# A two-dimensional DFT in array quadrants, and the engines' order from the scheduler's other machine model

## The chip, the cores and the metric

The kernel runs on one core of one Trainium2 chip. The metric is the device time of one execution in microseconds (us), smaller is better. A core has five engines that run side by side, each with its own instruction queue: TensorE (PE in the profile: matrix multiplications, whose weight loads are listed as PEld), VectorE (DVE), ScalarE (ACT), GpSimd (POOL), and SyncE (SP), which here only issues DMA transfers. An engine executes its queue in order. When its next instruction needs something that is not there yet, it waits, and everything behind that instruction waits with it.

## The reference, cut to what matters

The input is 32 images of 96 channels, 56 x 56 pixels, float32. Two layers follow one another.

```python
# layer 0
h = silu(bn(conv1x1(x, w1)))                 # 96 -> 576 channels
h = silu(bn(depthwise3x3(h, w2)))
s = sigmoid(w_b @ silu(w_a @ mean(h)))       # squeeze and excitation
x = x + bn(conv1x1(h * s, w3))               # 576 -> 96
# layer 1
mag = abs(rfft2(x))                          # first DFT
ca  = channel_attention(mag)                 # 96 numbers for an image
s   = stack(mean_c(x), l2_c(x), resize(mean_c(mag)))
s   = conv_1x15(conv_15x1(s))                # each of the 3 planes by itself
sa  = sigmoid(mix(relu(conv3x3(s))))         # one 56 x 56 map for an image
y   = x * ca * sa
freq_e = resize(mean_c(abs(rfft2(y))))       # second DFT
aux = concat(y, coord, freq_e)
offset, gate, base = conv3x3(aux), gate_net(aux), conv3x3(y)
z   = (1 - gate) * base + gate * deformable_conv3x3(y, offset)
out = relu(batchnorm_over_all_images(z) + x)
```

What the change touches is `abs(rfft2(.))`, computed twice for each image, 64 times in all, and the order in which the instructions of the whole kernel stand on four of the five engines.

## The kernel before

**Stages.** `body` (line 1332) calls `layers`, which computes everything up to z for all images, and then `normalise`, which reads z and x back, applies the batch normalisation and writes the output. A third function, `gather_block`, serves offsets too large for the fast path; with these inputs it is not executed.

**Three streams in `layers`.** The main loop goes over 224 bands (7 bands of 8 rows for each of 32 images), and over two halves of a band. A half loads its interpolation weights (`weights_load`, to `wc` and `wr`) and multiplies them (`weights`, VectorE, L685). `block_channels` copies 8 x 8 pixel blocks (GpSimd, L696), transposes them (TensorE, L700) and copies the result out (ScalarE, L702). `sample_tiles` interpolates the samples by matrix multiplication (TensorE, L714, ScalarE copies in L718), `pack` moves part of the samples to the spare partitions with three ScalarE copies (L725), and `deform` multiplies by the deformable kernel (TensorE, L733). The joint 3x3 convolution (L598), the base convolution (L626) and `combine` (VectorE, L772 to L775) complete the band. Between these pieces the loop steps two Python generators: `hidden`, which is layer 0 of the image two ahead (TensorE L166, ScalarE L170 and L219, VectorE L259), and `attend` for the image one ahead. So each image period holds work of three images.

**`attend` of an image.** It first projects (L321, after loads of the hidden rows `hq`). Then `dft_mag` takes the first DFT, `resized_spectrum` (L420 to L423) averages it over channels, L490 to L512 compute the channel attention, and L514 to L549 the spatial attention. The spatial part is a chain of small steps: L524, L526 and L527 on TensorE, L528 on ScalarE, three L533 with L534 on ScalarE, nine L540 with L542 on ScalarE, L544 and L546 on VectorE, L549 on TensorE, and the sigmoid (L273 on ScalarE, L274 on VectorE). Its result `sa` is sent to DRAM by a DMA of GpSimd's queue (L554), and is multiplied into the loaded pixels by GpSimd (L363, in `weigh`) for the second DFT. The row of frequency energy that follows goes to DRAM from L565 over L567 and L570 (`fqd`), and is loaded into the padded image by L589, a transfer of SyncE's queue, which the joint convolution L598 needs.

**`dft_mag`.** The 96 channels are taken as two halves of 48 that lie on the partitions side by side (2 x 56 = 112 rows of pixels). In six groups of eight channels a tile `x2` (112 x 8 x 56) is loaded. Four matmuls (L383) use two channels of `x2` as weights (112 columns) and a constant block matrix `FU` of 116 columns as the moving data: this is the DFT along one image axis. ScalarE copies the result to `s1` (L390). The transform along the other axis (L404) runs over `s1` in three steps. Each step has two parts (real and imaginary) of two matmuls that accumulate, with a 112 x 112 block-diagonal constant `GV` as weights and 464 moving columns. So in each of these matmuls half of the weights are zeros. ScalarE squares each part out of its accumulation bank (L406), and VectorE adds the two squares (L407). The square root (L410) ends the DFT. The tile `sq` of the squares and the tile `s1` have one buffer each, `x2` has three.

**What sets the order.** SyncE's queue is written out by hand: within `layers` the engine is under a manual schedule, so its transfers stand as the program emits them. The order on TensorE, VectorE, ScalarE and GpSimd is decided when the program is built. A list scheduler plays the emitted program on a model of the machine and writes, for each engine, the order in which instructions became ready; an earlier emission has the higher priority. The scheduler has two machine models with different costs, and before the change the default one is in use:

```python
    with tile.TileContext(nc) as tc:
```

Accumulation memory is shared among the streams: six banks for general use (`bank`, named `mm` in the profile), one (`acc`) for the small steps of the attention, one (`pd`) for `deform`.

Of the kernel before, what the change touches and what calls it, by code (L numbers as in the profile page):

```python
# [7 lines left out]
FP = mybir.dt.float32  # L8
I32 = mybir.dt.int32
AF = mybir.ActivationFunctionType  # L10
ALU = mybir.AluOpType
# [13 lines left out]
V = W // 2 + 1  # L25
# [35 lines left out]
NG = C // 2 // CG  # L61
KG = 3
# [52 lines left out]
def bank(p):  # L115
    return p["mm"].tile([128, 512], FP, name="mm")
# [219 lines left out]
def dft_mag(nc, p, src, gate=None):  # L336

    w = p["w"]
    hwc = src.rearrange("c (h w) -> h c w", h=H)
    s1 = p["s1p"].tile([2 * W, NP, 2 * V], FP, name="s1")
    if gate is None:
        parts = p["sq"].tile([2 * W, 2, NPB * V], FP, name="sq")[:, :, : NG * W].rearrange("p k (g w) -> p k g w", g=NG)  # L350
    x2s = []

    def load(g):
        if g < NG:
            x2 = p["x2"].tile([2 * H, CG, W], FP, name="x2")
            for half in range(2):
                c0 = half * C // 2 + g * CG
                nc.sync.dma_start(x2[half * H : (half + 1) * H], hwc[:, c0 : c0 + CG])
            x2s.append(x2)

    def weigh(g):
        if gate is not None and g < NG:
            nc.gpsimd.tensor_tensor(x2s[g], x2s[g], gate.unsqueeze(1).to_broadcast([2 * H, CG, W]), ALU.mult)  # L363

    def sums(g):
        sq = bank(p)[: 2 * H, : CG * W].rearrange("h (c w) -> h c w", c=CG)
        nc.scalar.activation(sq, x2s[g], AF.Square)
        for k, t in enumerate((x2s[g], sq)):
            nc.vector.tensor_reduce(parts[:, k, g], t.rearrange("h c w -> h w c"), AX.X, ALU.add)

    for g in range(3):
        load(g)
    for _ in range(2):
        yield
    weigh(0)
    weigh(1)
    yield
    if gate is not None:
        yield
    for g in range(NG):  # L380
        pt = bank(p)
        for i in range(CG // 2):
            nc.tensor.matmul(pt[: 2 * W, i * 4 * V : (i + 1) * 4 * V],  # L383
                             x2s[g][:, 2 * i : 2 * i + 2, :].rearrange("h c w -> h (c w)"), w["FU"],
                             start=True, stop=True)
        if gate is None:
            sums(g)
        weigh(g + 2)
        load(g + 3)
        nc.scalar.copy(s1.rearrange("p (h q) u -> p h q u", h=2)[:, :, g * CG // 2 : (g + 1) * CG // 2],  # L390
                       pt[: 2 * W, : 2 * CG * V].rearrange("p (q h u) -> p h q u", h=2, u=2 * V))
        yield
    if gate is None:
        p["sums"] = p["sp"].tile([2 * H, 2, W], FP, name="sums")
        nc.vector.tensor_reduce(p["sums"], parts.rearrange("p k g w -> p k w g"), AX.X, ALU.add)
    mag = s1[:, :, :V]
    for j in range(0, NP, NPB):
        n = NPB * V
        sq = p["sq"].tile([2 * W, 2, n], FP, name="sq")
        cos, sin = s1[:, j : j + NPB, :V], s1[:, j : j + NPB, V:]  # L400
        for part, first, second in ((0, (0, cos), (1, sin)), (1, (0, sin), (2, cos))):
            pt = bank(p)
            for k, (g, m) in enumerate((first, second)):
                nc.tensor.matmul(pt[: 2 * W, :n].rearrange("p (q u) -> p q u", q=NPB), w["GV"][:, g], m,  # L404
                                 start=(k == 0), stop=(k == 1))
            nc.scalar.activation(sq[:, part], pt[: 2 * W, :n], AF.Square)  # L406
        nc.vector.tensor_tensor(mag[:, j : j + NPB], sq[:, 0].rearrange("p (q u) -> p q u", q=NPB),  # L407
                                sq[:, 1].rearrange("p (q u) -> p q u", q=NPB), ALU.add)
        yield
    nc.scalar.activation(mag, mag, AF.Sqrt)  # L410
    p["magnitude"] = mag


def resized_spectrum(nc, p, mag, name, scale=None):


    m2 = p["sp"].tile([2 * W, V], FP, name=f"m_{name}")
    if scale is not None:
        nc.vector.tensor_tensor(mag, mag, scale.unsqueeze(2).to_broadcast([2 * W, NP, V]), ALU.mult)
    nc.vector.tensor_reduce(m2, mag.rearrange("p q u -> p u q"), AX.X, ALU.add)  # L420
    yield
    pf = p["acc"].tile([128, 512], FP, name="acc")
    nc.tensor.matmul(pf[:V, : 2 * W], m2, p["w"]["RT2"], start=True, stop=True)  # L423
    rs = p["sp"].tile([V, 2, W], FP, name=name)
    nc.scalar.copy(rs.rearrange("p m w -> p (m w)"), pf[:V, : 2 * W])
    p["resized"] = rs
    yield


def attend(tc, p, b, x, h2d, pooled, x1, given=False):  # L430
# [45 lines left out]
    mas = p["sp"].tile([2 * W, 2, NP], FP, name="mas")  # L476
    edge = p["sp"].tile([2 * W, NP, NE], FP, name="edge")
# [3 lines left out]
    for m in range(2):  # L481
        we = p["sp"].tile([2 * W, NP, NE], FP, name="we")
        nc.vector.tensor_tensor(we, edge, w["wa"][:, m], ALU.mult)
        nc.vector.tensor_reduce(mas[:, m], we, AX.X, ALU.add)


    qs = p["sp"].tile([2 * W, 2, 3, NP], FP, name="qs")
    for m in range(2):
        nc.vector.tensor_tensor(qs[:, m], mas[:, m].unsqueeze(1).to_broadcast([2 * W, 3, NP]), w["wb"][:, m], ALU.mult)
# [16 lines left out]
    c2 = p["sp"].tile([2 * MID, 2 * W], FP, name="c2")  # L506
# [5 lines left out]
    nc.tensor.matmul(pc[: 2 * W, 64 : 64 + NP], c2, w["cp2X"], start=True, stop=True)  # L512
    cx = p["sp"].tile([2 * W, NP], FP, name="cx")
    nc.vector.tensor_tensor(cx, pc[: 2 * W, 64 : 64 + NP], w["cp2bX"], ALU.add)  # L514
# [264 lines left out]
def constants(tc, ctx, a, p, gather=False):  # L779
# [63 lines left out]
    wa = cp.tile([2 * W, 2, NP, NE], FP, name="wa")  # L843
    wb = cp.tile([2 * W, 2, 3, NP], FP, name="wb")
    gb = cp.tile([C, 3], FP, name="gbias")
    with tc.tile_pool(name="l1w", bufs=1) as wp:
# [7 lines left out]
        ap, bp, fdh, fdw = temp("apad", 2 * W), temp("bpad"), temp("fdhX"), temp("fdwX")  # L854
        ta = wp.tile([2 * W, NP, NE], FP, name="ta")
        tb = wp.tile([2 * W, 3, NP], FP, name="tb")
        for m in range(2):
            for d in range(7):
                first = d == 0
                oa, ob = (wa[:, m], wb[:, m]) if first else (ta, tb)  # L860
                nc.vector.tensor_tensor(oa, ap[:, m, d].unsqueeze(1).to_broadcast([2 * W, NP, NE]),
                                        fdh[:, :, d : d + 1].to_broadcast([2 * W, NP, NE]), ALU.mult)
                nc.vector.tensor_tensor(ob, bp[:, m, :, d : d + 1].to_broadcast([2 * W, 3, NP]),
                                        fdw[:, :, d].unsqueeze(1).to_broadcast([2 * W, 3, NP]), ALU.mult)
                if not first:
                    nc.vector.tensor_tensor(wa[:, m], wa[:, m], ta, ALU.add)
                    nc.vector.tensor_tensor(wb[:, m], wb[:, m], tb, ALU.add)
# [41 lines left out]
def padded(nc, p, a, images):  # L909
# [3 lines left out]
    for t in yps:  # L913
        nc.gpsimd.memset(t, 0.0)
        nc.sync.dma_start(t[C : C + 4, PD : PD + H, PD : PD + W], a["coord"])
        nc.sync.dma_start(t[CA:, PD : PD + H, PD : PD + W], a["place"])
    p["s4"] = [cp.tile([H, 3, WP], FP, name=f"s4_{i}") for i in range(2)]
# [11 lines left out]
def layers(tc, a, dp, x1d, zd, stats, far):  # L929
# [8 lines left out]
    with ExitStack() as ctx:  # L938
# [7 lines left out]
        pools(tc, ctx, p, None, (("xt", 2), ("acch", 2), ("pl", 2), ("w3s", 1), ("hq", 1), ("o", 2), ("x2", 3),  # L946
# [290 lines left out]
def gather_block(tc, a, dp, x1d, zd, stats):  # L1237
# [4 lines left out]
    with ExitStack() as ctx:  # L1242
# [11 lines left out]
        pools(tc, ctx, p, None, (("x2", 3), ("ca", 1), ("s1p", 1), ("xc", 2), ("sp", 1), ("sq", 2), ("q1", 2), ("q2", 2),  # L1254
# [95 lines left out]
def _arrays(inp):  # L1350
# [39 lines left out]
    A["cp1"] = np.ascontiguousarray(cp1.reshape(2 * MID, 3, NP, 2).transpose(2, 1, 3, 0))  # L1390
    cp2 = l1["cp2_w"].reshape(NP, 2, MID)
    A["cp2X"] = np.ascontiguousarray(cp2.transpose(1, 2, 0).reshape(2 * MID, NP))
    A["cp2bX"] = np.ascontiguousarray(np.repeat(l1["cp2_b"].reshape(NP, 2).T, W, 0))
    A["twoT"] = np.kron(np.eye(2), np.ones((MID, W))).astype(f)
# [8 lines left out]
    for k in range(1, KA):  # L1403
# [13 lines left out]
    A["GV"] = np.ascontiguousarray(np.stack(  # L1417
        [np.kron(two, np.cos(t)), np.kron(two, np.sin(t)), np.kron(two, -np.sin(t))], 1).astype(f))
    A["two"] = np.kron(two, np.ones((W, 1))).astype(f)
# [8 lines left out]
    apad, bpad = np.zeros((1, 2, 7, V), f), np.zeros((2, W, 2, 3, 7), f)  # L1428
    for d in range(7):
# [3 lines left out]
        bpad[:, -np.arange(V), 1, :, d] = bp[:, 6 - d : 6 - d + V].T[:, None]  # L1433
# [4 lines left out]
    A["apad"], A["bpad"] = ends, bpad.reshape(2 * W, 2, 3, 7)  # L1438
    A["bsum"] = np.stack([bp[:, 6 - d : 6 - d + V].sum(1) for d in range(7)], -1).astype(f)[None]
    pairs = lambda v: np.repeat(v.reshape(NP, 2, 7).transpose(1, 0, 2), W, 0)  # L1440
# [7 lines left out]
    RT2 = np.zeros((2, W, 2, W), f)  # L1448
    RT2[:, np.arange(V), 0] = RT / C
    RT2[:, -np.arange(V), 1] = RT / C  # L1450
    A["RT2"] = RT2.reshape(2 * W, 2 * W)
# [37 lines left out]
```

## Time and profile before

| quantity | value |
|---|---|
| time, median of 3 runs | 9672.42 us (9670.12 to 9673.45) |
| the profiled execution's own time | 9701.68 us |
| its span | 9699.9 us |
| TensorE busy | 8626.3 us, 89% of the span |
| VectorE busy | 7237.3 us, 75% |
| ScalarE busy | 5341.9 us, 55% |
| GpSimd busy | 2531.2 us, 26% |
| granted TensorE clock, mean | 0.932 of full speed |
| column transform, L404 | 662.9 us busy, 1536 records |
| row transform, L383 | 418.1 us busy, 3072 records |

How to read it: the profile is of one execution, and its span is the sum that all its rows belong to; it lies 29 us above the median of the runs that were timed without a profile. [...] A row of a group of instructions reads: line, engine, operation, tile written and tiles read, shapes, number of records, then the busy time in us, the mean of one in ns, and the idle time of the engine just ahead of these instructions with what ended most of it. Records of matmuls overlap, so that a mean is longer than the pace at which they follow one another. A row of a timeline reads: start in us, duration in us, engine and operation with the number of records, and in brackets the idle time before it and what ended it. A row of the table by stretches gives, for each engine, busy us and the number of records, and at its end the granted clock, the share of the DMA engines' time that is busy, and GB/s. A row of the waits gives the us in all, how often, and the longest.

### The profile page before, as it was taken

Reading aid. Unit: us, or ns where it says so; the run is one execution under the profiler, and the core shown is the slowest. Engines: PE = TensorE matmul, PEld = TensorE weight load, DVE = VectorE, ACT = ScalarE, POOL = GpSimd, SP = SyncE. Lnnn points to the kernel's source line nnn. Section 1 sums busy time; section 2 is a strip of 40 time slices with the busy share of each in tenths; the row PEclk is TensorE's granted clock in tenths of the full one; section 3 lists DMA queues with packets and bytes.
Section 4 is the critical chain, followed back from the end, with each engine's and each line's share of the span. In section 5 each row is a group of like instructions: output and inputs, shape, how many; then the busy total and the mean of one; then the engine's idle time right before and its main releaser. Section 6 shows DMA issues by size and latency. Waiting matters only on the chain. (4 is left out here: it accounts for less than half of the span.)

```text
span 9699.9 us, 120622 instructions
## 1 busy us (share of the span) xinstructions
PE 8626.3 (89%) x43766; PEld 5004.7 (52%) x43766; DVE 7237.3 (75%) x6948; ACT 5341.9 (55%) x10262; POOL 2531.2 (26%) x2639
## 2 busy tenths in 40 slices
PE   6889999999999999999999999999999999999970
PEld 3455555555555555555555555555555555555540
DVE  7688777777877777787777787777778777777323
ACT  2355555555555556555555555555555555555453
POOL 0133222222222232222222222233222223322210
PEclk9899999999999999999999999999999999999985
DMA  2345555554555555555555555555545555554449
GB/s 94 107 136 143 160 153 157 157 153 138 140 158 152 157 149 148 140 144 150 153 158 154 139 139 155 153 157 155 152 138 143 151 157 157 153 146 135 128 152 417
DMA packets 1069310, 1485.39 MB, mean 153 GB/s; under 512 B 590406, under 2 KB 839958, under 8 KB 1056422
## 3 DMA queue, kind: packets, MB, share of 16 engines
q1 hardware_dynamic: 858747, 985.20, 37.3%
q10 hardware_dynamic: 153675, 329.79, 9.1%
q0 software_dynamic: 56288, 162.60, 6.8%
q8 instruction: 352, 5.77, 0.3%
q14 instruction: 248, 2.03, 0.1%
HBM read 1064.28 MB, written 412.65 MB: 152 GB/s over the span
## 5 line engine op out<-in xcount | busy, mean ns | idle before, releaser
L259 DVE SCALAR_TENSOR_TENSOR acch<-hp,w,acch 128x1512 f32<-128x1512 f32 (+1 forms) x2250 | 4314.4, 1918 | 32.8
L598 PE MATMUL mm<-yp,c_jointW 104*128 104x448 f32 x4032 | 1648.5, 561 | 6.2 <-DMA yp<-fqd 3.4
L733 PE MATMUL pd<-v,c_def 128*96 128x224 f32 (+1 forms) x6272 | 1435.2, 380 | 174.5 <-ACT v L725 147.9
L696 POOL COPY ybl<-yp 96x448 f32<-96x448 f32 x896 | 1016.6, 1161 | 2002.3 <-PE mm L700 1996.8
L733 PEld LDWEIGHTS pd<-v,c_def 128*96 128x96 f32 (+1 forms) x6272 | 1065.3, 175 | 487.7 <-ACT v L725 186.7
L166 PE MATMUL mm<-xt,w 96*128 96x392 f32 (+3 forms) x2688 | 1117.2, 553 | 132.6 <-ACT yt L702 95.9
L714 PE MATMUL mm<-wc,yt 64*96 64x144 f32 x12544 | 1113.9, 301 | 119.1 <-ACT v L718 59.3
L598 PEld LDWEIGHTS mm<-yp,c_jointW 104*128 104x128 f32 x4032 | 785.1, 196 | 802.7 <-issue 760.1
L685 DVE TENSOR_TENSOR wc<-wc,wr 128x1008 f32<-128x1008 f32 x448 | 559.3, 1248 | 776.4 <-DMA wr<-hd 767.9
L219 ACT ACTIVATE acch<-acch,sh,inv 128x1568 f32<-128x1568 f32 x288 | 487.4, 1692 | 1159.2 <-DVE acch L259 1141.5
L714 PEld LDWEIGHTS mm<-wc,yt 64*96 64x96 f32 x12544 | 847.7, 162 | 442.9 <-issue 197.7
L718 ACT COPY v<-mm 96x288 f32<-96x288 f32 (+1 forms) x2688 | 1003.1, 441 | 127.9 <-PE mm L714 85.6
L170 ACT ACTIVATE hp<-mm,sh,inv 128x392 f32<-128x392 f32 (+2 forms) x1216 | 811.6, 672 | 329.4 <-PE mm L166 280.8
L626 PE MATMUL mm<-yp,c_base0W 96*64 96x448 f32 x4032 | 914.6, 551 | 0.0
L321 PE MATMUL mm<-hq,w3s 128*96 128x392 f32 x2048 | 789.9, 532 | 126.5 <-DMA hq<-h2d 124.2
L648 POOL DMA_DIRECT2D od<-at x224 | 185.9, 830 | 2257.6 <-DVE at L644 1483.9
L725 ACT COPY v<-v 32x448 f32<-32x448 f32 x1344 | 755.1, 562 | 29.7
L404 PE MATMUL mm<-s,c_GV 112*112 112x464 f32 x1536 | 662.9, 573 | 0.0
L166 PEld LDWEIGHTS mm<-xt,w 96*128 96x128 f32 (+1 forms) x2688 | 390.5, 187 | 513.8 <-issue 289.8
L702 ACT COPY yt<-mm 128x384 f32<-128x384 f32 (+1 forms) x896 | 351.1, 441 | 463.9 <-PE mm L700 462.0
L321 PEld LDWEIGHTS mm<-hq,w3s 128*96 128x96 f32 x2048 | 336.9, 173 | 478.6 <-issue 374.4
L626 PEld LDWEIGHTS mm<-yp,c_base0W 96*64 96x64 f32 x4032 | 295.3, 135 | 527.8 <-issue 487.9
(193 smaller groups left out, 8959.1 us busy)
## 6 DMA issues: line engine op xcount, KB each, us to landing
h2d<-acch ACTq DMA_DIRECT2D x288, 784.0 KB
wc<-hd SPq DMA_DIRECT2D x896, 252.0 KB
wr<-hd SPq DMA_DIRECT2D x896, 252.0 KB
hq<-h2d SPq DMA_DIRECT2D x128, 980.0 KB
hq<-h2d SPq DMA_DIRECT2D x128, 784.0 KB
x<-x1d SPq DMA_DIRECT2D x768, 98.0 KB
ht<-od SPq DMA_DIRECT2D x224, 252.0 KB
hd<-ht ACTq DMA_DIRECT2D x224, 252.0 KB
```

The costliest lines, as they stand in the source:

```text
L166: nc.tensor.matmul(pt[p0 : p0 + w1.shape[1], : rows * W], w1, xts[hf][:, r0 * W : (r0 + rows) * W], start=True, stop=True)
L170: nc.scalar.activation(h1[lo:hi, row0 : row0 + rows, 1 : 1 + W], pt[lo:hi, : rows * W].rearrange("p (h w) -> p h w", h=rows), AF.Silu, bia ...
L259: nc.vector.scalar_tensor_tensor(acc[:, lo:hi], win, wk, acc[:, lo:hi], ALU.mult, ALU.add)
L321: nc.tensor.matmul(pts[half][:C, :EW], w3s[:, ch], hq, start=(i == 0), stop=False)
L404: nc.tensor.matmul(pt[: 2 * W, :n].rearrange("p (q u) -> p q u", q=NPB), w["GV"][:, g], m, start=(k == 0), stop=(k == 1))
L598: nc.tensor.matmul(view, weights[:, k], yp[:channels, r0 : r0 + RB, dx + PD - 1 : dx + PD - 1 + W], start=(k == 0), stop=(k == NTAP - 1))
L626: nc.tensor.matmul(pb[k % 2 * BC : (k % 2 + 1) * BC, :BW].rearrange("p (h w) -> p h w", h=RB), w["base"][:, k], yp[:C, r0 : r0 + RB, dx + ...
L696: nc.gpsimd.tensor_copy(yb[:, :, s], blocks)
L714: nc.tensor.matmul(pt[k][:C, (t - lo) * KP : (t - lo + 1) * KP], yt[ps, t], s[ps, t * KP : (t + 1) * KP], start=True, stop=True)
L718: nc.scalar.copy(v[:C, :, lo:hi, k].rearrange("c k t p -> c t k p"), pt[k][:C, : (hi - lo) * KP].rearrange("c (t k p) -> c t k p", t=hi - ...
L725: nc.scalar.copy(v[C:, 1 + 2 * i : 3 + 2 * i], v[i * QC : (i + 1) * QC, KA:])
L733: nc.tensor.matmul(out.rearrange("c q (t x) -> c t q x", x=TS), p["w"]["def"][ks, k], v[ks, k].rearrange("c t s (r x) -> c t (s r) x", r=T ...
```

## The change

It has two parts. The first is one argument in `kernel`: the list scheduler plays the program on its other machine model, so that the order on TensorE, VectorE, ScalarE and GpSimd is another one. SyncE's hand-written order stays.

The second is in `dft_mag`, with the constants that it needs. Each half of the channels now lies on 64 partitions instead of 56 (`WX`), of which the last eight are padding. The three `x2` tiles are no longer taken from a pool: they are three fixed tiles, zeroed once at the start by GpSimd and used in turn. The row transform's weights are 128 columns wide instead of 112. The column transform is divided into the four quadrants of the TensorE array: a matmul has 56 rows of one row half (`r`), writes 64 columns of one column half (`k`) and has 232 moving columns, so there are 48 of them for a DFT where there were 12, and no zero block. A step fills two banks, one for each row half, and one bank holds both parts. A square now covers one bank (464 columns, both parts), so there are still six squares and three additions for a DFT. The order of the channels changes with it, and the constants follow by `order`. The small tiles of the attention become 128 partitions high instead of 112.

```diff
+WX = 64
+NQB = 8
...
-    s1 = p["s1p"].tile([2 * W, NP, 2 * V], FP, name="s1")
+    s1 = p["s1p"].tile([2 * WX, NP, 2 * V], FP, name="s1")
...
-            x2 = p["x2"].tile([2 * H, CG, W], FP, name="x2")
+            x2 = p["x2"][p["n_x2"] % len(p["x2"])]
+            p["n_x2"] += 1
             for half in range(2):
                 c0 = half * C // 2 + g * CG
-                nc.sync.dma_start(x2[half * H : (half + 1) * H], hwc[:, c0 : c0 + CG])
+                nc.sync.dma_start(x2[half * H : (half + 1) * H, :, :W], hwc[:, c0 : c0 + CG])
             x2s.append(x2)
...
-            nc.tensor.matmul(pt[: 2 * W, i * 4 * V : (i + 1) * 4 * V],
+            nc.tensor.matmul(pt[:, i * 4 * V : (i + 1) * 4 * V],
...
     mag = s1[:, :, :V]
-    for j in range(0, NP, NPB):
-        n = NPB * V
-        sq = p["sq"].tile([2 * W, 2, n], FP, name="sq")
-        cos, sin = s1[:, j : j + NPB, :V], s1[:, j : j + NPB, V:]
-        for part, first, second in ((0, (0, cos), (1, sin)), (1, (0, sin), (2, cos))):
-            pt = bank(p)
-            for k, (g, m) in enumerate((first, second)):
-                nc.tensor.matmul(pt[: 2 * W, :n].rearrange("p (q u) -> p q u", q=NPB), w["GV"][:, g], m,
-                                 start=(k == 0), stop=(k == 1))
-            nc.scalar.activation(sq[:, part], pt[: 2 * W, :n], AF.Square)
-        nc.vector.tensor_tensor(mag[:, j : j + NPB], sq[:, 0].rearrange("p (q u) -> p q u", q=NPB),
-                                sq[:, 1].rearrange("p (q u) -> p q u", q=NPB), ALU.add)
+    n = NQB * V
+    pairs = mag.rearrange("p (r q) u -> p r q u", r=2)
+    for q0 in range(0, NP // 2, NQB):
+        sq = p["sq"].tile([2 * WX, 2, 2, n], FP, name="sq")
+        pts = bank(p), bank(p)
+        for part, first, second in ((0, (0, 0), (1, V)), (1, (0, V), (2, 0))):
+            for t, (g, u0) in enumerate((first, second)):
+                for r, k in ((0, 0), (1, 1), (0, 1), (1, 0)):
+                    rows = slice(r * WX, r * WX + W)
+                    q1 = k * NP // 2 + q0
+                    nc.tensor.matmul(pts[r][k * WX : (k + 1) * WX, part * n : (part + 1) * n].rearrange("p (q u) -> p q u", q=NQB),
+                                     w["GV"][rows, g], s1[rows, q1 : q1 + NQB, u0 : u0 + V], start=(t == 0), stop=(t == 1))
+        for r, pt in enumerate(pts):
+            nc.scalar.activation(sq[:, r].rearrange("p k n -> p (k n)"), pt[:, : 2 * n], AF.Square)
+        nc.vector.tensor_tensor(pairs[:, :, q0 : q0 + NQB], sq[:, :, 0].rearrange("p r (q u) -> p r q u", q=NQB),
+                                sq[:, :, 1].rearrange("p r (q u) -> p r q u", q=NQB), ALU.add)
         yield
     nc.scalar.activation(mag, mag, AF.Sqrt)
...
+    p["x2"], p["n_x2"] = [cp.tile([2 * H, CG, WX], FP, name=f"x2_{i}") for i in range(3)], 0
+    for t in p["x2"]:
+        nc.gpsimd.memset(t, 0.0)
     p["s4"] = [cp.tile([H, 3, WP], FP, name=f"s4_{i}") for i in range(2)]
     for t in p["s4"]:
         nc.gpsimd.memset(t, 0.0)
...
+    order = np.arange(C).reshape(2, NP // 2, 2).transpose(0, 2, 1).reshape(2, NP)
+    A["cp1"] = np.ascontiguousarray(cp1.reshape(2 * MID, 3, C)[:, :, order].transpose(3, 1, 2, 0))
...
-    A["GV"] = np.ascontiguousarray(np.stack(
-        [np.kron(two, np.cos(t)), np.kron(two, np.sin(t)), np.kron(two, -np.sin(t))], 1).astype(f))
-    A["two"] = np.kron(two, np.ones((W, 1))).astype(f)
+    gv = np.zeros((2, WX, 3, WX), f)
+    gv[:, :W, :, :W] = np.stack([np.cos(t), np.sin(t), -np.sin(t)], 1)
+    A["GV"] = gv.reshape(2 * WX, 3, WX)
...
-    with tile.TileContext(nc) as tc:
+    with tile.TileContext(nc, schedule_with_timeline_sim=True) as tc:
```

## The prediction

> **What bounds the kernel now.** I read the page first (busy totals, costly groups), then TensorE's waits, then its timeline round the two places that the change touches.
>
> ```profile
> PE 8626.3 (89%) x43766; PEld 5004.7 (52%) x43766; DVE 7237.3 (75%) x6948; ACT 5341.9 (55%) x10262; POOL 2531.2 (26%) x2639
> ...
> L733 PE MATMUL pd<-v,c_def 128*96 128x224 f32 (+1 forms) x6272 | 1435.2, 380 | 174.5 <-ACT v L725 147.9
> ...
> L404 PE MATMUL mm<-s,c_GV 112*112 112x464 f32 x1536 | 662.9, 573 | 0.0
> ```
>
> TensorE (PE) is busy 89% of the span. In the band loop, 600 to 9240 us, it is busy 8015.7 of 8640 us by the windows, so 624 us are idle, some 20 us in each image period of 285 us. VectorE is at 75% and the others are lower. The end, 9400 to 9700 us, is bound by DMA (417 GB/s in the last slice) and is untouched. So a microsecond off TensorE's work, or off its waits, in the loop is a microsecond off the time, as long as nothing new is waited for. The answers by line show what is waited for, and two rows that the change will meet:
>
> ```profile
> PE mm L321 <- DMA hq<-h2d: 124.2, 30, 7.9
> PE mm L166 <- ACT yt L702: 95.9, 40, 5.4
> ...
> PE mm L383 <- POOL x L363: 37.9, 35, 3.5
> ```
>
> ```profile
> L363 POOL TENSOR_TENSOR x<-x,sa 112x448 f32<-112x448 f32 x192 | 381.3, 2006 | 10.7 <-DMA x<-x1d 9.8
> ...
> L406 ACT ACTIVATE sq<-mm 112x464 f32<-112x464 f32 x384 | 202.3, 552 | 323.0 <-DVE s L407 235.9 <-PE mm L404 69.0 <-DVE sums L395 10.7
> ```
>
> **Part 1, the column transform in quadrants.** A float32 matmul leaves two records, and a burst of 16 records of L404 takes 6.59 us in the timeline: 0.412 us each. There are 64 DFTs (two for each of 32 images) x 24 records = 1536; 1536 x 0.412 = 633 us, all on TensorE's path. After: 64 x 48 instructions x 2 records = 6144 records of 232 columns instead of 464, so 0.206 us each. Four quadrants at once would make it 6144 / 4 x 0.206 = 316 us. One after another it would be 1266 us, two at a time 633. No quadrant pair stands in this trace; the nearest rows are two-way: L626 (two column halves) starts pairs some 7 ns apart every 381 ns, L714 (two row halves) pairs 6 ns apart every 122 ns, each the time of one. So halves do run together, in both directions. [...] By rows: a set of 16 new matmuls takes 16 x 2 / 4 x 0.206 = 1.65 us, and its evacuation two L406 squares (2 x 0.552) and one L407 addition (0.640), with hops some 2 us, through one single buffer. [...] Squares, additions and copies keep their number and size (112 to 128 partitions only), so they cost nothing new. Row transform: its weights grow from 112 to 128 columns. L700 loads 128 columns at a spacing of 82 ns, below L383's 97 to 99 ns, so the load stays hidden except at the head of a burst: 347 bursts x 15 ns = +5 us. Matmul time removed was also cover for other waits; a fifth of what is left of the gain: +40. Three tiles zeroed once at the start by GpSimd lie beside the first loads: 0. Sum -317 + 25 + 5 + 40 = **-247 us** (ends -300 and +10, the latter if quadrants run two by two).
>
> **Part 2, the other machine model.** It changes no instruction, only the order on TensorE, VectorE, ScalarE and GpSimd. SyncE's queue is in its hand-written order, so the loads keep theirs, except in the normalisation at the end (a few us, taken as 0). I compared the built programs' orders.
>
> *What is lost: the spatial attention's chain.* L524, L526, L527, L533 (3), L540 (9), L549, then L383 of the gated DFT is a chain PE-ACT-PE-ACT-PE-ACT-DVE-PE-ACT-DVE-POOL-PE. In the kernel before, from the third image on, other matmuls fill it. In the timeline of the third:
>
> ```profile
> 882.74 0.26 PE L527 MATMUL acc<-thM,fe 29*56 29x56 f32 x2
> ...
> 889.81 3.21 PE L598 MATMUL mm<-yp,c_jointW 104*128 104x448 f32 x8
> 892.96 0.40 PE L549 MATMUL acc<-sa,c_halves 56*112 56x56 f32 x2
> 893.28 4.08 PE L598 MATMUL mm<-yp,c_jointW 104*128 104x448 f32 x10
> ...
> 898.20 4.03 PE L626 MATMUL mm<-yp,c_base0W 96*64 96x448 f32 x18
> ...
> 902.92 0.96 PE L383 MATMUL mm<-c_FU,x 112*112 112x116 f32 x8
> ```
>
> From the end of L527 to the start of L383 are 19.92 us, of which 17.56 are other matmuls: the chain costs TensorE 2.36 us. In the changed program nothing stands between these on TensorE in any image after the first few: L527, 3 x L533, 9 x L540, L549, 4 x L383, one behind another. The price is shown by this trace's own first image, which is bare but for one matmul group:
>
> ```profile
> 312.01 0.26 PE L527 MATMUL acc<-thM,fe 29*56 29x56 f32 x2
> 312.20 1.68 PE L166 MATMUL mm<-xt,w 96*128 96x448 f32 x4
> ...
> 318.42 0.81 PE L540 MATMUL acc<-s,tv 56*56 56x56 f32 x6 [0.39 <-ACT r L542]
> 322.36 0.62 PE L549 MATMUL acc<-sa,c_halves 56*112 56x56 f32 x2 [3.13 <-DVE sa L546]
> 326.40 1.89 PE L383 MATMUL mm<-c_FU,x 112*112 112x116 f32 x8 [3.42 <-POOL x L363]
> ```
>
> 14.14 us, of which 1.61 are other work: 12.5 own. The new price is 12.5 - 2.36 = 10.1, and 0.9 more because the first L363 takes 1.1 us there and 2.0 in the mean: 11.0 us x 31 images = **+341 us**. In these stretches the clock falls too:
>
> ```profile
> 318.00:320.00 2.00, 0.84 (x7) 0.63 (x6) 2.00 (x3) 0.60 (x2) 0.00 (x0) 0.50 0.00 0
> ...
> 322.00:324.00 2.00, 0.62 (x2) 0.45 (x2) 0.31 (x2) 1.85 (x3) 0.00 (x0) 0.50 0.00 0
> ...
> 328.00:330.00 2.00, 2.00 (x8) 1.34 (x8) 0.00 (x0) 0.89 (x2) 1.51 (x3) 0.50 0.10 23
> ```
>
> Granted clock (third column from the end) 0.50, and still 0.50 at 328 to 330, though TensorE is full again; it returns at 332.5, 6 us after the chain's end. [...] I take 2.5 x 31 = **+78 us**.
>
> *Other new waits.* L565 to L589 to L598 (the frequency row goes through GpSimd's queue to DRAM and back through SyncE's) has 5.2 us of TensorE work over it instead of 8.2. Before, L598 came 12 to 13 us after L565 and waited once (3.4 us). I take 2 us x 31 = +60 (0 to 115), the thinner cover over L321's loads with it.
>
> *What is won.* Between the last L718 copy and the last of its three packs (L725), ScalarE has 1.53 us of foreign work in the mean before and 0.31 after, over 448 half bands. Of L733's 147.9 us I take 90 off. L166's and L714's waits on ScalarE (95.9 and 59.3) and those of the channel attention's small matmuls are partly relieved too: 35. Together **-125 us** (-60 to -220). And after a stall of 11 us the other engines have caught up, so waits just behind it vanish: -50.
>
> Sum of part 2: 341 + 78 + 60 - 125 - 50 = +304 us (ends +130 and +430). **Net: -247 + 304 = +57 us.** The profiled run was 9701.7 us (span 9699.9), so it would be 9759; the median of the runs is 29 lower, 9672.4, which gives 9730.
>
> **The rivals.**
> - *The chain is cheaper (faster).* Place: L527 to L383, 31 times. If the other engines, less loaded than in image 0, run it in 8 us and the clock is not halved, it costs 31 x 8 = 248 instead of 419: -171, so 9560. It decides below 11.0 us for chain and clock together, instead of my 13.5 (2.5 x 31 = 77 = 57 + the 0.2% bound of 19). For it: image 0 had a DVE L259 of 1.84 us in the way. Against it: the changed order has an L259 there again.
> - *Quadrants run two by two.* Part 1 becomes +10: 9672 + 10 + 304 = 9986. For it: the trace shows pairs only. Against it: pairs in both directions.
> - *The stall replaces waits.* TensorE idles 20 us per image already; if 3 us more of it than the 50 / 31 = 1.6 vanish behind the stall, -93: 9637, and anything up to no change. Against it: the large waits (L733, L321) are short reactions of ScalarE and DMA elsewhere in the image.
>
> **How the numbers follow.** Chances: mine 0.45 (9650 to 9830), cheap chain 0.27, two by two 0.16, replaced waits 0.12. Range 9550 to 9970, which leaves out about 0.1 on each side; by my own case alone 9650 to 9830. Faster by over 0.2% (19 us, about what a measurement of this kernel can tell from no change): 0.25 of the cheap chain and 0.05 of the replaced waits, 0.30. Within 0.2%: 0.09, from these two and the low end of mine. Slower: the rest, 0.61.
>
> **What would show it.** The column transform's group near 316 us of TensorE's pace, 16-matmul sets some 1.7 us long; if 3.3, quadrants are two by two. TensorE's waits: L546, L363, L534 and L542 (in their new lines) some 10 us an image where they had 2; granted clock 0.5 there, its mean under 0.932; L725's wait near 60. It is wrong if the chain's wait sums to under 200 us, or if another wait of over 100 us (the frequency row, the hidden rows) appears.

## The result, and the profile after

The changed kernel takes 11388.67 us (median of 4 runs, 11353.96 to 11390.36) against 9672.94 us for the kernel before on the same chip: a ratio of 1.1768, 95% interval 1.1751 to 1.1785. It is slower, as forecast, but by 1716 us instead of 57, and far outside the range. The ratios below are all to the kernel before as it ran beside each kernel.

Lines of the changed kernel are numbered 2 to 7 higher than before: 166 is 168, 321 is 323, 363 is 366, 383 is 386, 404 is 410, 406 is 413, and from 423 on seven more (685 is 692, 733 is 740). In kernels with an imposed order, two or three more are added.

The page of the changed kernel, its totals and the groups that answer to those shown of before:

```profile
span 11352.2 us, 129768 instructions
...
PE 9209.7 (81%) x48374; PEld 5557.1 (49%) x48374; DVE 7051.4 (62%) x6948; ACT 5362.0 (47%) x10267; POOL 2053.3 (18%) x2642
...
L692 DVE TENSOR_TENSOR wc<-wc,wr 128x1008 f32<-128x1008 f32 x448 | 543.5, 1213 | 2549.0 <-DMA wr<-hd 2487.7
...
L740 PE MATMUL pd<-v,c_def 128*96 128x224 f32 (+1 forms) x6272 | 1516.6, 395 | 2.0 <-ACT v L725 2.0
...
L410 PE MATMUL mm<-s,c_GV 56*64 56x232 f32 x6144 | 493.9, 438 | 162.6 <-ACT sq L413 161.0
```

The span is 1652 us longer. TensorE is busy 583 us more, although its column transform is shorter, and idle 2142 us instead of 1074. Two things that the prediction counted as gains are there: L410 is shorter than L404 was, and the wait of L733 for the packs, 147.9 us, has shrunk to 2.0. But the third line is new in size: now VectorE stands 2487.7 us in front of the product of the interpolation weights for its loads. Before, it stood there 767.9 us:

```profile
DVE wc L685 <- DMA wr<-hd: 767.9, 164, 17.7
```

VectorE has no longer work than before, and is idle 4301 us of the span.

TensorE's waits of the changed kernel (us in total, times, longest):

```profile
PE mm L323 <- ACT v L732: 305.8, 29, 13.3
PE mm L721 <- DVE yb L638: 283.8, 138, 7.2
PE mm L410 <- ACT sq L413: 161.0, 27, 12.4
PE mm L707 <- DVE sq L372: 143.2, 15, 11.0
PE mm L323 <- DMA hq<-h2d: 105.4, 29, 8.4
PE mm L386 <- POOL x L366: 97.5, 36, 6.1
PE acc L501 <- DVE qs L497: 90.8, 14, 6.8
```

Of the seven, three wait for VectorE directly, and L410 waits for it over ScalarE: L413 itself stands for VectorE's addition L414 (496.1 us, before 235.9). L721 waited for the same sum of the base convolution 39.4 us before. The first row is a wait for VectorE too, though the profile names ScalarE's pack L732. L323 also needs the scaled weights `w3s`, which VectorE writes in L296, and in all 29 stands it starts 0.10 us after L296 has ended. In one of them the way from the product to TensorE can be followed:

```profile
2099.18 1.21 DVE L692 TENSOR_TENSOR wc<-wc,wr 128x1008 f32<-128x1008 f32 x1 [12.45 <-DMA wr<-hd]
2101.45 0.21 ACT L293 ACTIVATE s<-s 128x5 f32<-128x5 f32 x1 [11.72 <-DVE s L292]
2104.92 0.65 DVE L296 TENSOR_TENSOR w3s<-w,s 128x480 f32<-128x480 f32 x1
2105.67 2.90 PE L323 MATMUL mm<-hq,w3s 128*96 128x392 f32 x4 [12.09 <-ACT v L732]
```

VectorE stands 12.45 us at the product. Behind it, in its queue, are L292, for which ScalarE waits (330.0 us in all), and L296, for which TensorE waits.

The timeline of the changed kernel at another stand, first SyncE's issues of the loads (start, duration), then VectorE:

```profile
2738.54 0.61 SPq L685 DMA_DIRECT2D wc<-hd  x1
2739.24 0.59 SPq L686 DMA_DIRECT2D wr<-hd  x1
2739.88 0.57 SPq L685 DMA_DIRECT2D wc<-hd  x1
2740.51 0.60 SPq L686 DMA_DIRECT2D wr<-hd  x1
```

```profile
2739.48 6.00 DVE L261 SCALAR_TENSOR_TENSOR acch<-hp,w,acch 128x1568 f32<-128x1568 f32 x3
2750.94 1.21 DVE L692 TENSOR_TENSOR wc<-wc,wr 128x1008 f32<-128x1008 f32 x1 [5.47 <-DMA wr<-hd]
2752.07 3.62 DVE L261 SCALAR_TENSOR_TENSOR acch<-hp,w,acch 128x1512 f32<-128x1512 f32 x2
```

The last of four loads is issued at 2740.51, and the product starts at 2750.94, 10.4 us later. VectorE was there at 2745.5 and stood 5.5 us; nothing behind the product could start. In the kernel before, in contrast, a last load and its product, which had nothing to wait for when VectorE reached it 14.3 us after the issue:

```profile
2295.72 0.57 SPq L679 DMA_DIRECT2D wr<-hd  x1
2309.97 1.21 DVE L685 TENSOR_TENSOR wc<-wc,wr 128x1008 f32<-128x1008 f32 x1
```

Over the image loop I measured on both traces, for each product, the time from the issue of its last load to VectorE's arrival, and to the start where it had to wait:

| kernel | issue to arrival, median us | issue to start where it waited | stands over 0.3 us | wait at the product, us, whole program |
|---|---|---|---|---|
| before | 11.1 | 10.6 | 134 of 390 | 767.9 |
| after | 5.2 | 10.2 | 348 of 390 | 2487.7 |

The loads did not become slower. VectorE comes six microseconds earlier, at half the time that they take.

The clock carries a part of the loss. Its mean is 0.849 instead of 0.932; as it is either 1 or 0.5 in the traces (158 stretches at 0.5 before, 281 after; a mean between them is of a stretch that has both), TensorE ran at half clock for some (1 - 0.849) x 2 x 11352 = 3430 us, before 1320.

### The profile page after: what moved, and what is told of

It reads as the page before. It is cut to its first block, busy times and chain, and to the rows that moved or that the text cites. A ratio compares the mean times of both kernels' runs of the same rounds, so it can differ in the third digit from the quotient of the medians.

```text
span 11352.2 us, 129768 instructions
## 1 busy us (share of the span) xinstructions
PE 9209.7 (81%) x48374; PEld 5557.1 (49%) x48374; DVE 7051.4 (62%) x6948; ACT 5362.0 (47%) x10267; POOL 2053.3 (18%) x2642
## 5 line engine op out<-in xcount | busy, mean ns | idle before, releaser
L261 DVE SCALAR_TENSOR_TENSOR acch<-hp,w,acch 128x1512 f32<-128x1512 f32 (+1 forms) x2250 | 4188.5, 1863 | 29.5
L692 DVE TENSOR_TENSOR wc<-wc,wr 128x1008 f32<-128x1008 f32 x448 | 543.5, 1213 | 2549.0 <-DMA wr<-hd 2487.7
L721 PE MATMUL mm<-wc,yt 64*96 64x144 f32 x12544 | 1403.7, 327 | 359.5 <-DVE yb L638 283.8
L740 PE MATMUL pd<-v,c_def 128*96 128x224 f32 (+1 forms) x6272 | 1516.6, 395 | 2.0 <-ACT v L725 2.0
L721 PEld LDWEIGHTS mm<-wc,yt 64*96 64x96 f32 x12544 | 1093.9, 180 | 754.2 <-DVE yb L638 327.4
L740 PEld LDWEIGHTS pd<-v,c_def 128*96 128x96 f32 (+1 forms) x6272 | 1118.6, 184 | 369.7 <-issue 144.9
L725 ACT COPY v<-mm 96x288 f32<-96x288 f32 (+1 forms) x2688 | 1038.3, 439 | 532.9 <-PE mm L721 504.8
L323 PE MATMUL mm<-hq,w3s 128*96 128x392 f32 x2048 | 850.2, 565 | 423.6 <-ACT v L732 305.8
L703 POOL COPY ybl<-yp 96x448 f32<-96x448 f32 x896 | 704.8, 814 | 2253.3 <-PE mm L707 2253.0
L172 ACT ACTIVATE hp<-mm,sh,inv 128x392 f32<-128x392 f32 (+2 forms) x1216 | 815.2, 674 | 591.8 <-PE mm L168 485.5
L732 ACT COPY v<-v 32x448 f32<-32x448 f32 x1344 | 755.1, 562 | 28.9
L323 PEld LDWEIGHTS mm<-hq,w3s 128*96 128x96 f32 x2048 | 359.6, 185 | 826.2 <-issue 454.4
L410 PE MATMUL mm<-s,c_GV 56*64 56x232 f32 x6144 | 493.9, 438 | 162.6 <-ACT sq L413 161.0
L386 PE MATMUL mm<-c_FU,x 112*128 112x116 f32 x3072 | 489.6, 312 | 135.5 <-POOL x L366 97.5
```

The source lines that it names most:

```text
L172: nc.scalar.activation(h1[lo:hi, row0 : row0 + rows, 1 : 1 + W], pt[lo:hi, : rows * W].rearrange("p (h w) -> p h w", h=rows), AF.Silu, bia ...
L261: nc.vector.scalar_tensor_tensor(acc[:, lo:hi], win, wk, acc[:, lo:hi], ALU.mult, ALU.add)
L323: nc.tensor.matmul(pts[half][:C, :EW], w3s[:, ch], hq, start=(i == 0), stop=False)
L692: nc.vector.tensor_tensor(wc, wc, wr, ALU.mult)
L703: nc.gpsimd.tensor_copy(yb[:, :, s], blocks)
L721: nc.tensor.matmul(pt[k][:C, (t - lo) * KP : (t - lo + 1) * KP], yt[ps, t], s[ps, t * KP : (t + 1) * KP], start=True, stop=True)
```

## Experiments

Two theories stood at first. **A**: the stand at the product, with all that is behind it on VectorE, makes the loss. **B**: TensorE's own order, with the bare chain of the prediction. Later **D**: the stand is only where lateness shows, and VectorE's order as a whole is at fault.

**The two parts by themselves.**

```diff
 # quadrants_alone: the changed kernel
-    with tile.TileContext(nc, schedule_with_timeline_sim=True) as tc:
+    with tile.TileContext(nc) as tc:
 # planner_alone: the kernel before
-    with tile.TileContext(nc) as tc:
+    with tile.TileContext(nc, schedule_with_timeline_sim=True) as tc:
```

> The quadrants, with the engines' order from the default machine model as in the kernel before. All theories: the column transform's sets take 1.85 us in the changed kernel's trace against 3.3 us before, so 192 sets save 192 x 1.45 = 278 us at full clock, less some cover; 9400 to 9480 us. If it were over 9672 us, the quadrants themselves would be part of the loss.

Measured: 9663.46 us, ratio 0.9988 (0.9977 to 1.0000). The quadrants win nothing that counts, and the expectation is missed by some 180 us. The groups of this kernel:

```profile
L410 PE MATMUL mm<-s,c_GV 56*64 56x232 f32 x6144 | 375.7, 377 | 1.8 <-ACT sq L413 1.8
...
L386 PE MATMUL mm<-c_FU,x 112*128 112x116 f32 x3072 | 468.1, 302 | 53.2 <-POOL x L366 34.2 <-DMA x<-x1d 14.5 <-DVE sq L372 4.4
...
L707 PE MATMUL mm<-c_ident,ybl 96*128 96x96 f32 x3136 | 357.6, 250 | 92.2 <-ACT sq L413 86.8 <-POOL ybl L703 4.5 <-DVE sq L372 0.9
```

The column transform is 287 us shorter (662.9 to 375.7), as expected. But the row transform is 50 us longer (418.1 to 468.1), the transposes L707 stand 92.2 us instead of 13.2, and more small waits and slower clocks take the rest. Summed over all groups, TensorE is busy 149 us less and idle 110 us more. So of the 287 us, 50 are in the row transform, about 88 in the other matmuls (the mean clock is 0.922 instead of 0.932), and 110 are idle time.

> The DFT of the kernel before, with the order from the other machine model. Both theories: all of the loss is in the order, so the loss stays and the quadrants' gain is missing: 11500 to 11750 us. If it is below 11000 us, the two parts together lose more than each by itself.

Measured: 11488.06 us, 1.1888 (1.1854 to 1.1922). The whole loss is in the order. Beside it the changed kernel, 11388.67 us, is 1.0% faster: that is what the quadrants are worth on this order.

**One engine's order at a time.** Both models order the same instructions, so an engine's order can be recorded from one program and imposed on another, by edges that ask for order of issue and no wait. The rest is then ordered by the program's own model. With one engine held, TensorE, where it isn't the one, keeps 88 to 93% of its pairs of neighbours, the others 55 to 83%; so a run changes more than the engine named, and is no price of that engine's order by itself. ScalarE in the run with VectorE's order imposed on the default program, for one, keeps 57% of the neighbours that it has in the quadrants alone, where the two models' own programs share 50% (by the starts in the traces).

```diff
+def impose(tc, engine, text):
+    ...
+    mine = [i for i in tc.nc.cur_bb.bb.instructions if i.engine == engine]
+    ...
+        tc.add_manual_dep(have[b], have[a].name, mybir.DependencyInfo(mybir.DependencyClass.NoSync, mybir.DependencyReason.DATA),
+                          reason="order")
 ...
         layers(tc, a, dp, x1d, zd, stats, far)
+    impose(tc, mybir.EngineType.DVE, ORDER_DVE)
```

> The changed kernel, but VectorE's instructions stand in the order that the default model gave; the other engines are still ordered by the other model. Theory A (VectorE comes to the product of interpolation weights, L692, about 5 us too early and stands there for its loads, and all behind it is late): the wait at L692 falls from 2488 us to below 1000, and the time to 9700 to 10200 us. Theory B (TensorE's own order is the cause, with its bare chain of the spatial attention and others like it): under 300 us are won, the time stays above 11000 us.

Measured: 10761.60 us, 1.1143 (1.1115 to 1.1170). The wait at the product falls to 815.2 us and 627 us are won: more than B allows and less than A expected.

```profile
DVE wc L694 <- DMA wr<-hd: 815.2, 132, 17.9
DVE z L781 <- PE pd L742: 490.1, 36, 23.4
DVE sa L553 <- ACT r L551: 441.0, 31, 19.6
```

VectorE now waits elsewhere, for the deformable bank and for the spatial attention. That the others' order fits another VectorE is a likely reason, which no run isolates.

> The changed kernel, but TensorE's instructions stand in the order that the default model gave; the other engines are still ordered by the other model. Theory A: the bare chain is filled again, worth 8.2 us x 31 = 255 us and some clock, and the wait at L692 stays above 1800 us: 10900 to 11150 us. Theory B: most of the loss is gone, 9450 to 10000 us.

Measured: 11173.44 us, 1.1553 (1.1515 to 1.1592). 215 us are won, fewer than A expected even for the chain; the wait at the product stays at 2168.5. B falls as the main cause.

The mirror images, on the good background:

> The quadrants with the default model's order, except that VectorE's instructions stand in the order of the other model. Theory A: VectorE waits over 1800 us at L692 and the time is 10200 to 10600 us, against 9663 with the default order. If VectorE's order hurts only together with TensorE's, below 9900.

> The quadrants with the default model's order, except that TensorE's instructions stand in the order of the other model: the bare chain alone. Priced by the changed kernel's trace it costs 10.6 us an image instead of 2.4, 8.2 x 31 = 254 us, and with the clock that it halves some 60 more: 9900 to 10050 us. By theory B (TensorE's order is the main cause) above 10500.

> The quadrants with the default model's order, except that ScalarE's instructions stand in the order of the other model, with the three packs behind one another. By the prediction's step 90 us are won at L740's wait: 9560 to 9650 us. If ScalarE's eager order does as VectorE's does, above 9800.

Measured: 11300.98 us (1.1666, 1.1646 to 1.1685), 10170.01 us (1.0513, 1.0493 to 1.0533) and 10080.34 us (1.0410, 1.0392 to 1.0427). With VectorE's order imposed, and what that moves on the others, nearly the whole loss comes, 1638 us over the quadrants alone and more than expected. Its waits:

```profile
DVE wc L694 <- DMA wr<-hd: 2087.1, 304, 18.5
DVE z L781 <- PE pd L742: 436.7, 35, 15.7
```

The other two runs cost 507 and 417 us over the quadrants alone. The first is more than expected; there VectorE also stands 1145.7 us at the product (716.3 with the default order), so it isn't the chain alone. The second is the other case of its expectation, above 9800: ScalarE's order, which I had counted as a gain for the packs, is a loss. The three sum to far more than the whole loss, so they can't be added. TensorE's order is worth 215 us on the other model's program and 507 on the default one; that the orders are made for one another is a reading of this. GpSimd's order was held by itself in no run.

**The stand itself.** Here the product multiplies a constant instead of what was loaded. The loads go on, to tiles that nothing reads; their buffers no longer wait for the product. The order of the changed kernel is kept (VectorE's imposed, over 99% of neighbours the same on the others). The samples are left without their weights.

```diff
 def weights_load(nc, p, hd, h):
-    wc = p["wc"].tile([2 * NS, NTH * KP], FP, name="wc")
-    wr = p["wr"].tile([2 * NS, NTH * KP], FP, name="wr")
+    wc, wr = (p["wr"].tile([2 * NS, NTH * KP], FP, name="wr") for _ in range(2))
 ...
-def weights(nc, wc, wr):
-    nc.vector.tensor_tensor(wc, wc, wr, ALU.mult)
+def weights(nc, p):
+    wc = p["wc"].tile([2 * NS, NTH * KP], FP, name="wc")
+    any_ = p["w"]["ident"][:, :NTH * 16].unsqueeze(1).to_broadcast([2 * NS, KP // 16, NTH * 16])
+    nc.vector.tensor_tensor(wc.rearrange("p (a b) -> p a b", a=KP // 16), any_, any_, ALU.mult)
```

> The changed kernel with the same order on every engine, but the product L692 multiplies a constant by itself and so waits for no load; the loads are still made, to tiles that nothing reads (the interpolation is left without its weights). Theory A (VectorE's stand at L692 for its loads is the main cause): its 2488 us of waits are gone and the time falls by 900 us or more, to 10500 or below. Theory D (the stand is only the place where a late VectorE or a late SyncE shows, and the order itself is at fault): less than 300 us are won, above 11050.

Measured: 10079.39 us, 1.0417 (1.0399 to 1.0434). VectorE's row at the product:

```profile
L695 DVE TENSOR_TENSOR wc<-c_ident 128x1008 f32<-128x1008 f32 x448 | 546.7, 1220 | 0.0
```

1309 of the 1716 us are gone. This is A, and D, which allowed under 300, falls. The loads' buffers come free earlier here as well; the next two runs leave the loads as they were.

**The place of the product alone.** In the recorded order of VectorE, only the products are moved.

```diff
 # in the recorded order, for each product (the first and last images excepted)
-L692  L261  L261  L779
+L261  L261  L779  L692
```

> The changed kernel with the other model's order, except that each product L692 stands some 4 us of VectorE's work later in VectorE's queue (412 of 448 of them, the first and last images excepted). Theory A: the wait at L692 falls from 2488 to 1000 to 1400 us and the time by 500 to 900 us, to 10500 to 10900. Theory D (the order of the rest is at fault): less than 200 us.

> The same with 8 us instead of 4: by theory A the wait falls below 700 us and the time to 10100 to 10500, towards the 10079 of the run without the wait. If L692 now comes too late for the samples, TensorE's waits show L692 (they had 7.7 us), and the time rises again.

Measured: 10665.13 us (1.1013, 1.0987 to 1.1040) and 10293.91 us (1.0635, 1.0608 to 1.0662). VectorE's waits at the product, of the first and of the second:

```profile
DVE wc L694 <- DMA wr<-hd: 757.7, 174, 17.9
```

```profile
DVE wc L694 <- DMA wr<-hd: 301.3, 47, 18.2
```

With the arrival 11.6 us and 16.3 us after the issue (means; after had 5.2), the stand shrinks and the time with it: 724 and then another 371 us, 1095 together. The first wait fell further than expected. In the second run some 17 of the 301.3 us are left in the image loop; the rest is at products that were not moved. Here too the order on the other engines is nearly that of the changed kernel (TensorE keeps 94 and 93% of its neighbours, ScalarE 92 and 90).

**The same step on the default order.** The kernel before already stood at 164 of its products. The products that waited are moved later, by as much as they waited, up to 6 us.

> The quadrants with the default model's order, and the products L692 that waited there (118 of 448) moved later by as much as they waited, up to 6 us. By theory A VectorE wins some 400 us of its stands (731 us before); as VectorE has slack in the default order, TensorE's waits on VectorE (70.8, 42.6 and 39.4 us) are all there is to win: 9570 to 9660 us. If it is still 9663, the stand costs nothing where VectorE has slack.

> The kernel before (its DFT and the default model's order), with the products L685 that waited there (130 of 448) moved later by as much as they waited, up to 6 us; it is to be set beside the quadrants with the same step, 9455 us. If the 2.4% of that run are the product's place alone, this one is at 9440 to 9480 too. If both parts add up (the quadrants' 280 us of matmul time come through once VectorE does not stand), it is at 9550 to 9680.

Measured: 9454.84 us, 0.9764 (0.9742 to 0.9786), and 9530.58 us, 0.9866 (0.9845 to 0.9886). The second lies between its two expectations, nearer to the parts adding up. So the product's place is worth 1.3% in the kernel before, and the quadrants another 1.0% on top, where they were worth 0.1% without it: between 75 us (by the medians) and 100 (by the ratios), which is a third of what the column transform saves. The first of the two is the fastest kernel of the study; its expectation had thought that only TensorE's direct waits on VectorE were to be won, which was too little. The groups of the quadrants with the product later show where the rest came from:

```profile
L412 PE MATMUL mm<-s,c_GV 56*64 56x232 f32 x6144 | 365.4, 369 | 1.0 <-ACT sq L415 1.0
L709 PE MATMUL mm<-c_ident,ybl 96*128 96x96 f32 x3136 | 343.6, 247 | 6.2 <-POOL ybl L705 3.5 <-ACT sq L415 1.3 <-DVE yb L640 0.7
```

The transposes' wait for ScalarE's squares, 86.8 us in the quadrants alone, is 1.3. The squares had not been slow (551 ns each in both). They waited for VectorE's addition, 265.3 us in the quadrants alone and 99.0 here; and before each of these waits of the transposes, 25 in the trace, VectorE had stood at a product within the last 6 us.

**The bare chain by itself.** On the default order, 23 matmuls an image are moved out of the chain between L534 and L556:

```diff
 # in TensorE's recorded order, images 2 to 31
-L534  (others)  L540 x3  (others)  L547 x9  (others)  L556
+L534  L540 x3  L547 x9  L556  (others)
```

> The quadrants with the default model's order, but on TensorE the spatial attention's steps L540, L547 and L556 stand directly behind L534 in 30 images, with the 23 matmuls that lay between them moved behind L556; the rest of the chain, L556 to L386, keeps its cover. By the changed kernel's trace this stretch takes 7.6 us when bare against some 2 us of its own work when filled: 5.5 x 30 = 165 us, and the clock that falls 1 to 2.5 us each, 30 to 75: 9860 to 9900 us, if the prediction's price of a bare chain is right. If TensorE wins back behind the stall what it lost in it (the prediction took 50 us of this), 9750 to 9810; if the stall costs nothing because other waits go, 9660 to 9700.

Measured: 9758.51 us, 1.0096 (1.0077 to 1.0115), which is 1.0108 times the quadrants alone, 105 us, give or take some 20. From the end of L534 to the end of L556, less other matmuls, TensorE took 2.4 us before and 8.4 us now: some 178 us in 30 images. So about two fifths are won back elsewhere.

## Why the prediction was wrong, point by point

*The bound.* "A microsecond off TensorE's work, or off its waits, in the loop is a microsecond off the time, as long as nothing new is waited for": the condition failed at once. The quadrants took 287 us off L404 and the time hardly moved: 50 us came back in the row transform, 88 as slower matmuls and 110 as idle time. Part of the last is VectorE's stands: with the products later 1.0% came through, a third. The rest of what was lost is not explained run by run. TensorE is the busiest engine, but it goes on only when what it needs is there, and in the changed kernel VectorE's stands decide that.

*The column transform.* 316 us were predicted, four quadrants at once. The -317 was my assumption: the trace of before has pairs only, and what the runs showed is -287 (the quadrants alone). A set of 16 matmuls (32 records) takes 1.85 us in the timeline, not 1.65, and the group is 375.7 us. Four quadrants do run together, since two by two would take the 3.3 us of before. That end is excluded.

*The wider weights*, +5 us, were mis-sized: 50 us. I took L700's spacing of 82 ns as proof that 128 columns load within it. Within its bursts L383's records follow at 99 ns before, and L386's at 112 after (medians); 13 ns for each of 3072 records are 40 us of the 50. L700 was no measure for it: its transposes leave one record each (3136 for 448 x 7), where L383's matmuls leave two (3072 for 64 x 24). Why its records follow at 82 ns with 128 columns, no run here shows.

*The evacuation*, +25 us, is a term that no run shows. In the quadrants alone L410 itself waits 1.8 us for the squares that empty its banks. L707's wait there, grown from 13.2 to 92.2 us, looks like a price of the evacuation; the run with the products later shows that it isn't that: with the same evacuation the wait is 6.2.

*The chain*, +341 us. It is bare as predicted. The timeline of one image of the changed kernel:

```profile
1648.77 0.26 PE L534 MATMUL acc<-thM,fe 29*56 29x56 f32 x2
...
1653.69 0.81 PE L547 MATMUL acc<-s,tv 56*56 56x56 f32 x6 [0.39 <-ACT r L549]
1656.33 0.62 PE L556 MATMUL acc<-sa,c_halves 56*112 56x56 f32 x2 [1.83 <-DVE sa L553]
1659.59 2.06 PE L386 MATMUL mm<-c_FU,x 112*128 112x116 f32 x8 [2.64 <-POOL x L366]
```

It takes 10.6 us instead of 12.5 (from L534 to L386, in most images), so 8.2 more than before: 254 us in all. (The prediction's 17.56 us of other matmuls are 17.8 by the trace, so that before it was nearer 2.1 than 2.36; this moves the sum by some 8 us.) L366 runs in 1.14 us at the median here, where I had added 0.9 for its mean of 2.0. And of the part that a run isolates, up to L556, 59% reached the time. The mechanism is right; if the same share holds for the rest of the chain, the term was about twice too large.

*The clock*, +78 us, was far too small, and no run shows the 2.5 us a chain that it takes. The stretches of the changed kernel round the same chain:

```profile
1652.00:1656.00 4.00, 1.71 (x13) 1.27 (x12) 3.90 (x6) 1.69 (x4) 0.55 (x1) 0.50 0.14 43
1656.00:1660.00 4.00, 1.03 (x4) 0.85 (x5) 0.46 (x2) 1.30 (x3) 2.17 (x3) 0.50 0.51 201
1660.00:1664.00 4.00, 4.00 (x25) 3.77 (x26) 0.00 (x0) 1.43 (x3) 3.63 (x6) 0.50 0.30 57
1664.00:1668.00 4.00, 4.00 (x28) 3.28 (x29) 2.03 (x2) 3.62 (x9) 1.46 (x3) 0.81 0.38 111
```

Around this place it behaves as in the first image of before: by the last row it is at half for 1.5 us more, until about 1665.5, 5.9 us after L386 starts, where the prediction's row has 6 us. Over the 32 images of the changed kernel's trace the clock is at half round this place in all, for 13.65 us and until 5.3 us after the start of L386 (medians); in the kernel before, in the first two alone. But the term counted one chain an image, and TensorE has more gaps of this kind, the stand of L323 shown above among them (half clock from 2095.6 to 2109.2). TensorE is busy 9209.7 us, where the same matmuls with the default order take 8476.8: 733 us of the loss are time in which TensorE is busy for longer with them, beside 959 us more of idle time than in that kernel (2142 against 1184).

*The frequency row*, +60: TensorE's wait for it is 29.0 us (10 times), before 3.4. Half. *The packs*, -90: the wait went from 147.9 to 2.0, more than predicted. What this is worth in the time no run isolates: ScalarE's whole order, put on the default program, costs 417 us. *The stall wins back*, -50: in the run with the bare chain it did, some 73 of 178 us; for the whole kernel no run shows it.

*What was missing* is the term that decides. Part 2 compared the orders on TensorE and, for the packs, on ScalarE, and asked for each matmul how much other TensorE work covers its wait. It put no price on VectorE's queue, though the page of before has the row of L685 with 767.9 us of waits for `wr`, 164 times: there is little margin at that place, and a move forward is paid in waits. Its own sign of being wrong, another wait of over 100 us on TensorE, came true with L323 (305.8), L721 (283.8), L410 (161.0) and L707 (143.2). The prediction asked what is queued behind a waiting instruction for TensorE and not for VectorE. Its three rivals had all the same limit, so the range ended 1400 us short. By the run without the wait, this term is 1309 us, and the moves of the product alone win 1095; the rest is 407 us by the first. How the rest divides between the orders of TensorE, ScalarE, GpSimd and what else VectorE has in another place stays open: TensorE's and ScalarE's cost more apart (507 and 417) than what is left of them together.

Why the other model puts the product so early is only argued: if it takes these loads to land in some 5 us, the list scheduler places the product as soon as it thinks them there. VectorE's other early waits point the same way (L592 stands 327.5 us for `sab` and 224.1 us for `yp`, both loads). No run shows the model's own numbers.

## What to carry to other kernels

When an order on in-order queues is changed, look on every engine, and not only on the busiest, at the instructions that are fed by DMA: take from the trace how long the loads need from their issue, and how long after the issue the engine arrives. Where these two are equal, as here (10.6 and 11.1 us), the engine is one step from standing, and moving the instruction a few microseconds later is worth a try before anything is made faster: it gave 1.3% by itself, and let a third of a saving on another engine come through. And where the profile names one releaser for a wait, as with L323, look at what else the instruction reads.

## What the runs showed of the hardware

Four float32 matmuls in four quadrants of the array run together: 16 of 232 columns take 1.85 us, where the 4 of 464 columns that they replace took half of the 6.59 us that a burst of 16 records took before, 3.3 us: 1.8 times faster for the same transform, half of whose weights had been zeros. For matmuls of 116 moving columns, widening the weights from 112 to 128 columns took the spacing of records from 99 to 112 ns. And half clock came with the stalls: round the bare chain the clock was at half for 13.65 us at the median of 32 images, and against the quadrants alone, 959 us of added idle time came with 1920 us more at half clock (0.849 of 11352 us against 0.922 of 9660), and TensorE was busy 733 us longer with the same matmuls.
